# Attention and convolution on one core: GpSimd in program order, the first inner sums of a projection made in the one ahead of it, and parts of k's weights prepared over a longer stretch

## The chip, the cores and the metric

The kernel runs on one core of a Trainium2 chip. The metric is the device time of one execution in microseconds (us), and the median over runs is compared. TensorE (PE in the profile) multiplies, VectorE (DVE), ScalarE (ACT) and GpSimd (POOL) work on elements, and SyncE (SP) and GpSimd issue the transfers between the memory outside the core (DRAM here) and the core's own (SBUF). PSUM holds the sums that TensorE makes.

## The reference

Four images of 1024 channels and 32 x 32 pixels, that is four batches of 1024 tokens, go through an attention layer and then through a convolution block. All is float32.

```python
x = hidden_states.reshape(B, C, N).transpose(0, 2, 1)
qkv = (x @ w_qkv.T + b_qkv).reshape(B, N, 3, nh, hd)
q, k, v = (qkv[:, :, 0], qkv[:, :, 1], qkv[:, :, 2])
q = _rmsnorm(_apply_rope(q, cos, sin).reshape(B, N, inner), q_norm_w).reshape(B, N, nh, hd)
k = _rmsnorm(_apply_rope(k, cos, sin).reshape(B, N, inner), k_norm_w).reshape(B, N, nh, hd)
attn = jax.nn.softmax(jnp.einsum('bqhd,bkhd->bhqk', q, k) * scale, axis=-1)
out = jnp.einsum('bhqk,bkhd->bqhd', attn, v).reshape(B, N, inner) @ w_proj.T
out = _rmsnorm(out, norm_out_w) + x
...
out = relu(_bn(_conv(out1, w1, b1, 1, 0), g1, be1))
out = relu(_bn(_conv(out, w2, b2, 1, 1), g2, be2))
out = relu(out1 + softplus(residual_scale)[0] * _bn(_conv(out, w3, b3, 1, 0), g3, be3))
```

The second part is a 1x1, a 3x3 and a 1x1 convolution with batch norms over all four images. It lies after everything that the change touches.

## The kernel before, in words

**Stages.** For each batch b = 0 to 3 TensorE works through five stages: the projections q, k and v, the attention, and the output projection, which the profile calls y (its sums are p_y). Below, q_1 is the q projection of batch 1, and so on. The convolutions come after y_3.

**Projections.** A 1024 x 1024 x 1024 product is done with seven products of halves in place of eight (Strassen's scheme in Winograd's form). For b = 0 that is one level, `project`: 28 units of 8 matmuls, weights from `operands` (L224), which makes sums of weight blocks on VectorE and stores them in a DRAM tensor wd (L242). For b > 0 each of the seven products is again done with seven, `project2` (L422): 49 products of 8 matmuls. k = 0 to 6 counts the seven outer ones. Their weight parts were prepared once, by `prepare` (L400): it loads four quarters, makes four sums on VectorE (`make`, L407 to L410) and stores them into the DRAM tensor wd2 (L412) through GpSimd's queue. The parts for q, v and y are prepared in the attention of batches 0 and 1; those for k (outer 1 to 6) in y_0, by lines L1015 and L1016, every 4 units, with `make` 3 units after the loads. Their temporaries are `big_temp` tiles, of which there are three; the rotation of q and k (`rope`) and the inverses of the softmax use the same three.

**Inner sums.** Each outer product also needs four sums of the right-hand operand, t1 to t4 (`inner`, L453; VectorE instructions L457 to L461). For k = 0 they stand at the start of the projection, for k + 1 they are made during k. `room` says where they lie, `spare` where partial results of the last two outer products lie. For q and k both are parts of a tile with 16 units (`beside`, L651); it is the tile of y's right-hand sums of the batch before, called `room`, `to` in the profile. `room(k)` there returns almost the same four units for every k. v is a tile of its own, allocated under the same tag "v" in a pool with one buffer (L604), so it takes the memory of `to` once that is released; its inner sums lie in v itself (`in_place`).

**Weights in flight.** Weight parts are loaded by SP into a ring of eight chunks of 256 KB (`wring`), seven per outer product, so a load can be issued when the product seven or eight places before it is through.

**Normalization and residual.** `o_norm` scales y (L818), eight tiles of 128 x 1024 elements for one batch, and stores each into the DRAM tensor x1d through GpSimd's queue (L819). This happens in the stage q of the next batch. The residual, x of that batch, is then added to x1d by transfers that add in DRAM (L976 with `accum_op`, GpSimd's queue, eight of 512 KB). In the program's text these stand at the head of the attention of the next batch, after v.

**What sets the order.** PE's order is that of the program (`manual_schedule`, L91); so is the order of VectorE and ScalarE from L928 on. The order on GpSimd and SP is made by a scheduler with a cost model. `after(n, step)` puts a step n products later in the text, `waiting` holds steps that are let in as VectorE has room, and `product_done` counts.

Of the kernel before, what the change touches and what calls it, by code (L numbers as in the profile page):

```python
# [11 lines left out]
F32 = mybir.dt.float32  # L12
AF = mybir.ActivationFunctionType
ALU = mybir.AluOpType
# [4 lines left out]
P = 128  # L19
B, C, H, W = 4, 1024, 32, 32  # L20
N = H * W
# [64 lines left out]
def program(ctx, tc, x, wblk, w2, w3, vecs, cos, sin, out, bad):  # L86
# [1 line left out]

    nc = tc.nc
    u = "f" if bad is not None else "s"  # L90
    ctx.enter_context(tc.manual_schedule(engines={mybir.EngineType.PE}))  # L91

    const = ctx.enter_context(tc.tile_pool(name=f"const{u}", bufs=1))
    dram = ctx.enter_context(tc.tile_pool(name=f"dram{u}", bufs=1, space=DRAM))
# [58 lines left out]
    with tc.tile_pool(name=f"st{u}", bufs=2) as st, ExitStack() as s:  # L153
# [61 lines left out]
        def flat(t):  # L215
            return t.rearrange("p a b -> p (a b)")
# [34 lines left out]
        def spend(cost):  # L251
            pace["room"] -= cost

        def after(n, step):
            later.append((pace["at"] + n, step))
# [133 lines left out]
        def quarter(t, base, k, oq, iq):  # L389
# [8 lines left out]
            nc.sync.dma_start(t.rearrange("p (g f) -> p g f", g=2), src.rearrange("g p f -> p g f"))  # L398

        def prepare(which, base, k, alloc):  # L400

            a11, a12, a21, a22 = a = alloc(f"pre_{which}_{k}")
            for i, t in enumerate(a):
                quarter(t, base, k, i // 2, i % 2)

            def make():
                nc.vector.tensor_tensor(a22, a21, a22, ALU.add)  # L407
                nc.vector.tensor_tensor(a21, a11, a21, ALU.subtract)
                nc.vector.tensor_tensor(a11, a22, a11, ALU.subtract)
                nc.vector.tensor_tensor(a12, a12, a11, ALU.subtract)  # L410
# [11 lines left out]
        def project2(b, which, base, right, room, spare, dest, tokens, tag, ready):  # L422

# [26 lines left out]
            def b_(k, iq, tq):  # L450
                return right(k, iq, tq)

            def inner(k, part):  # L453
                t1, t2, t3, t4 = t_[k] = room(k)
                spend(2 * TT)
                if part == 0:
                    nc.vector.tensor_tensor(t1, b_(k, 0, 1), b_(k, 0, 0), ALU.subtract)  # L457
                    nc.vector.tensor_tensor(t2, b_(k, 1, 1), t1, ALU.subtract)
                else:
                    nc.vector.tensor_tensor(t3, b_(k, 1, 1), b_(k, 0, 1), ALU.subtract)  # L460
                    nc.vector.tensor_tensor(t4, b_(k, 1, 0), t2, ALU.subtract)  # L461

            def bank2(kind, name):
                return bank(kind, name).rearrange("p (q e) -> p q e", q=2)
# [49 lines left out]
                after(2 * H2, lambda: add_to(k, 0, 0, o))  # L514
                product_done(H2)

            inner(0, 0)
            inner(0, 1)
            start(0)
            second(0)  # L520
            for k in range(len(OUTER)):
                more = k + 1 < len(OUTER)

                pace["hold"] = tokens and not more
                o = banks_[k][0]
                mm(o, w[k][2], t_[k][1], False, False)
                nc.scalar.copy(part(k, 0, 1), o)
                product_done(H2)
                ob = banks_[k][2] = bank2("o2", f"p5_{n}_{k}")
                mm(ob, w[k][3], t_[k][0], True, False)  # L530
                p5 = temp(f"p5_{n}_{k}").rearrange("p (q e) -> p q e", q=2)
                nc.scalar.copy(p5, ob)
                product_done(H2)
                if more:
                    start(k + 1)
                    inner(k + 1, 0)
                mm(o, w[k][4], t_[k][2], False, False)
                nc.scalar.copy(part(k, 1, 1), o)  # L538
                after(2 * H2, lambda k=k, p5=p5: add_to(k, 1, 1, p5))
                product_done(H2)  # L540
                if more:
                    second(k + 1)
                    inner(k + 1, 1)
                mm(ob, w[k][5], b_(k, 1, 1), False, True)
                after(2 * H2, lambda k=k, ob=ob: add_to(k, 0, 1, ob))
                product_done(H2)
                mm(o, w[k][6], t_[k][3], False, True)
                if k > 4:
                    after(2 * H2, lambda k=k, o=o: add(target(k, 1, 0), target(k, 1, 0), o))
# [9 lines left out]
        def qk_proj(b, base, bs, ts, bias, dst, tag, w1=None, two=None, bias_later=False):  # L559
# [36 lines left out]

                    after(0.5 * (i // 2 + 1), done)

            project2(b, two[0], base, two[1], two[2], two[3], dst, False, tag, ready)
            return total  # L600

        def v_proj(b, bs, ts, two=None):

            v = kv.tile([P, N // P, C], F32, tag="v", name=f"v_{b}")  # L604
            if two is not None:
                project2(b, 1, WV, two(v)[0], two(v)[1], two(v)[2], v, True, "v", lambda c: None)
                return v
# [8 lines left out]
            return v  # L616

        def operand(bs, ts):

# [28 lines left out]

            return right, room, spare

        def beside(bs, ts, units):  # L651


            def room(k):
                return units[12], units[13], units[14], units[15 if k % 2 == 0 else 0]

            def spare(k, oq, tq):
                return units[1 + k % 2] if (oq, tq) == (0, 1) else units[3 + oq]

            return operand(bs, ts), room, spare  # L660

# [261 lines left out]
        def v_room(name):  # L923
            return kv.tile([P, N // P, C], F32, tag="v", name=name)

        vector_and_act = {mybir.EngineType.DVE, mybir.EngineType.Activation}
        regions = ExitStack()
        regions.enter_context(tc.manual_schedule(engines=vector_and_act))  # L928
# [10 lines left out]
        queue_sums(ts[0], xs[0])  # L939
        room = v_room("rq_0")  # L940
        for b in range(B):
            units = [flat(room[:, i // 2 : i // 2 + 1, :])[:, half[i % 2]] for i in range(16)]
            units = [t.rearrange("p (q e) -> p q e", q=2) for t in units]
            q_all = kv.tile([P, NT, N], F32, tag="q", name=f"q_{b}")
            two = (0, *beside(xs[b], ts[b], units)) if b > 0 else None
            tq = qk_proj(b, WQ, xs[b], ts[b], "bq", q_all, "q", w1 if b == 0 else None, two, True)
            rope(b, q_all, tq, eps_q, HD / C, None, "q", b == 0)
            k_all = kp.tile([P, NT, N], F32, tag="k", name=f"k_{b}")
            two = (3, *beside(xs[b], ts[b], units)) if b > 0 else None
            tk = qk_proj(b, WK, xs[b], ts[b], "bk", k_all, "k", None, two)  # L950
            rope(b, k_all, tk, eps_rms, 1.0 / C, (wqk_other, wqk), "k")
            v = v_proj(b, xs[b], ts[b], (lambda v, b=b: in_place(xs[b], ts[b], v, True)) if b > 0 else None)

            rest(leave=4 if b > 0 else 0)
            psum_for("att")
# [41 lines left out]
            if b + 1 < B:  # L997
                xs[b + 1] = x_tile(b + 1)
                ts[b + 1] = t_tiles(b + 1)
                rows = (0, 1, 4, 5, 2, 3, 6, 7)  # L1000
                for j in range(NT):

                    def load(b=b, i=rows[j]):
                        for c in range(NCH):
                            load_x(b + 1, c, (i,))

                    after(3 + 1.5 * j, load)
                for i in range(0, NH, 2):
# [368 lines left out]
```

## Time and profile before

| what | value |
|---|---|
| median of 3 runs | 2767.21 us (2765.55 to 2784.42) |
| the profiled execution's own time | 2769.46 us |
| its span | 2767.7 us |
| granted TensorE clock, mean | 0.993 |
| busy: PE, DVE, ACT, POOL | 98%, 76%, 39%, 14% |
| transfers: SP's queue (q1), GpSimd's queue (q0) | 36.2%, 16.3% of 16 engines' span |

The starts of the stages on TensorE, in us from the span's start, are read from the sequence of matmuls in the timeline:

| batch | q | k | v | attention | y |
|---|---|---|---|---|---|
| 0 | 4.91 | 104.11 | 201.01 | 302.66 | 535.99 |
| 1 | 647.38 | 739.76 | 826.57 | 915.37 | 1148.69 |
| 2 | 1233.47 | 1329.24 | 1416.06 | 1504.04 | 1737.37 |
| 3 | 1822.15 | 1919.18 | 2005.99 | 2095.60 | 2329.51 |

The convolutions begin at 2414.22. Names in the profile: p_q, p_k, p_v and p_y are the sums of the projections, pa, pb and pc those of batch 0; sc and cx are the two matmuls of the attention, den the sums of its exponentials on VectorE, ks and qs the rotated halves of k and q, in flight to be added to k and q. "SPq" is the time for which SP is held at an issue of a transfer.

### The profile page before, as it was taken

What the parts mean: (1) busy time and instruction counts of PE and PEld (TensorE: products, weight loads), DVE (VectorE), ACT (ScalarE), POOL (GpSimd) and SP (SyncE); (2) the same over time, 40 slices, a digit from 0 to 9 for tenths busy, and PEclk for the clock granted to TensorE, in tenths of its full rate; (3) what the DMA queues carried; (4) which work ended last, traced back from release to release, by engine and by line L of the source; (5) the groups of instructions that cost most, each with busy time, mean ns of one, the idle gap of its engine ahead of it and who ended that gap; (6) DMA issues with size and microseconds to landing.
All of it is one profiled execution on the core that took longest, in us unless ns stands there. A gap on an engine that the chain in (4) does not pass through costs nothing.

```text
span 2767.7 us, 32938 instructions
## 1 busy us (share of the span) xinstructions
PE 2702.5 (98%) x11746; PEld 1657.4 (60%) x11746; DVE 2095.3 (76%) x2406; ACT 1080.2 (39%) x1494; POOL 383.6 (14%) x447
## 2 busy tenths in 40 slices
PE   9999999989999999999999999999999999999997
PEld 4449533337888433587887333887885335846853
DVE  4355599866688899886788877986888887646987
ACT  1221455413343555432343555232424554212266
POOL 1023023221111122101111110101111111000000
PEclk9999999999999999999999999999999999999999
DMA  5376254586867335359666210668674113672165
GB/s 206 107 186 187 84 168 152 172 307 202 229 189 212 86 111 164 114 169 247 184 187 173 62 24 16 198 193 212 189 218 121 24 24 98 193 261 88 62 215 212
DMA packets 242860, 432.05 MB, mean 156 GB/s; under 512 B 27072, under 2 KB 122608, under 8 KB 242688
## 3 DMA queue, kind: packets, MB, share of 16 engines
q1 hardware_dynamic: 209312, 318.59, 36.2%
q0 software_dynamic: 33376, 111.27, 16.3%
q8 instruction: 96, 1.57, 0.2%
q14 instruction: 76, 0.62, 0.1%
HBM read 295.22 MB, written 96.78 MB: 142 GB/s over the span
## 4 chain that ended last, share of the span: by engine, by line
PE 88%; DMA 5%; DVE 2%; ACT 2%; issue 1%; SPq 0%; POOL 0%; POOLq 0%; DVEq 0%; ACTq 0%
PE sc L758 16%; PE cx L775 16%; PE p_y L448 9%; PE p_v L443 8%; PE p_q L448 8%; PE p_k L448 7%; PE c L847 4%; PE c L1281 4%; PE pa_v L312 2%; PE pa_q L304 2%; DMA w_q<-wdf 2%; PE pa_k L304 2%; PE c2x L1142 2%; PE c2y L1142 2%; PE dn L796 1%
## 5 line engine op out<-in xcount | busy, mean ns | idle before, releaser
L769 DVE TENSOR_TENSOR den<-den,p 128x1024 f32<-128x1024 f32 x384 | 470.5, 1225 | 40.4 <-ACT p L765 0.5
L765 ACT ACTIVATE p<-sc 128x1024 f32<-128x1024 f32 x512 | 476.1, 1045 | 55.7 <-PE sc L758 55.7
L758 PE MATMUL sc<-q,k 64*128 64x512 f32 x2048 | 457.1, 596 | 3.0 <-DVE v L475 2.3
L775 PE MATMUL cx<-p,v 128*64 128x512 f32 x2048 | 453.6, 595 | 0.0
L758 PEld LDWEIGHTS sc<-q,k 64*128 64x128 f32 x2048 | 191.2, 186 | 266.8 <-issue 121.5
L775 PEld LDWEIGHTS cx<-p,v 128*64 128x64 f32 x2048 | 141.4, 137 | 304.3 <-issue 304.3
L739 POOL TENSOR_SCALAR q<-q,vec 128x512 f32<-128x512 f32 x64 | 127.3, 1995 | 537.0 <-DVE q L738 537.0
L780 ACT COPY q<-cx 128x512 f32<-128x512 f32 x64 | 37.5, 586 | 357.3 <-PE cx L775 357.3
L443 PE MATMUL p_v<-w_v,x 128*128 128x256 f32 x696 | 157.5, 379 | 0.2 <-DMA w_v<-wdf 0.2
L448 PE MATMUL p_y<-q,w_y 128*128 128x256 f32 x696 | 157.5, 380 | 0.0
L448 PE MATMUL p_k<-to,w_k 128*128 128x256 f32 x672 | 153.1, 381 | 2.3 <-ACT k L538 1.5
L448 PE MATMUL p_q<-to,w_q 128*128 128x256 f32 x672 | 153.9, 382 | 0.0
L448 PEld LDWEIGHTS p_y<-q,w_y 128*128 128x128 f32 x696 | 131.8, 190 | 20.7 <-issue 2.5
L443 PEld LDWEIGHTS p_v<-w_v,x 128*128 128x128 f32 x696 | 132.1, 190 | 18.8 <-DMA w_v<-wdf 0.9
L448 PEld LDWEIGHTS p_k<-to,w_k 128*128 128x128 f32 x672 | 126.7, 190 | 23.5 <-ACT to L538 2.8
L448 PEld LDWEIGHTS p_q<-to,w_q 128*128 128x128 f32 x672 | 128.8, 192 | 19.4 <-issue 1.6
L767 DVE TENSOR_TENSOR den<-p 128x1024 f32<-128x1024 f32 x64 | 76.5, 1195 | 76.0 <-ACT p L765 76.0
L802 DVE RECIPROCAL rec<-dn 128x512 f32<-128x512 f32 x32 | 107.2, 3349 | 14.4 <-PE dn L796 14.4
L1281 PE MATMUL c<-h,w 128*128 128x512 f32 x256 | 110.3, 592 | 0.9 <-ACT h L1185 0.9
L705 POOL DMA_DIRECT2D q<-qs x64 | 55.7, 1020 | 289.5 <-issue 170.7
L705 POOL DMA_DIRECT2D k<-ks x64 | 55.3, 1002 | 264.4 <-ACT p L765 104.9
L1281 PEld LDWEIGHTS c<-h,w 128*128 128x128 f32 x256 | 48.6, 190 | 62.1 <-issue 54.3
(521 smaller groups left out, 4183.8 us busy)
## 6 DMA issues: line engine op xcount, KB each, us to landing
wd2f<-w_pre POOLq DMA_DIRECT2D x88, 256.0 KB, 2.8
w_q<-wd2f SPq DMA_DIRECT2D x84, 256.0 KB
w_k<-wd2f SPq DMA_DIRECT2D x84, 256.0 KB
w_v<-wd2f SPq DMA_DIRECT2D x84, 256.0 KB
w_y<-wd2f SPq DMA_DIRECT2D x84, 256.0 KB
x<-in_x_dram SPq DMA_DIRECT2D x64, 256.0 KB
q<-qs POOLq DMA_DIRECT2D x64, 256.0 KB, 5.4
k<-ks POOLq DMA_DIRECT2D x64, 256.0 KB, 4.2
```

The lines of the kernel that those rows point to most:

```text
L304: nc.tensor.matmul(o, w[:, i, :], r(i), start=first and i == 0, stop=last and i == NH - 1, skip_group_check=True,)
L443: nc.tensor.matmul(o[:, q].rearrange("p (g f) -> p g f", g=2), r[:, i, q * P : (q + 1) * P], wt[:, :, i, :], skip_group_check=True, **at,)
L448: nc.tensor.matmul(o[:, q], wt[:, q, i, :], r[:, i, :], skip_group_check=True, **at)
L705: nc.gpsimd.dma_start(dst[i::2, f, :], other[1 - i :: 2, :], accum_op=ALU.add)
L739: nc.gpsimd.tensor_scalar(cx, cx, col("bv", hp), None, ALU.add)
L758: nc.tensor.matmul(sc[:, j], k_all[d, hp, t * P : (t + 1) * P], q_all[d, hp, at], start=True, stop=bad is not None,)
L765: nc.scalar.activation(p, sc, AF.Exp)
L769: nc.vector.tensor_tensor(d_, d_, p, ALU.add)
L775: nc.tensor.matmul(o[j * HD : (j + 1) * HD, :], v[:, t, h0 : h0 + HD], probs[t][:, j], start=(t == 0), stop=(t == N // P - 1),)
L847: nc.tensor.matmul(o, w[f][ih][:, ii, :], ys[:, i, half[c]], start=(i == 0), stop=(i == NT - 1))
L1142: nc.tensor.matmul(o[:, r * TR * TC : (r + 1) * TR * TC], uw[2 * h + r, j][:, i * PL + f * P : i * PL + (f + 1) * P], vt[b, i][:, 2 * h + ...
L1281: nc.tensor.matmul(os[i], w3t[k][f // NH][:, f % NH, :], h2[b, k][:, half[c]], start=(k == 0), stop=(k == NPT - 1),)
```

## The change

- GpSimd too is held to the program's order (the first hunk).
- Inner sums: `inner_sums` is taken out of `project2`. The sums for k = 0 of a projection are made in the last outer product of the projection ahead, through the list `ahead`: those of q in y of the batch before, those of k in q, those of v in k. A projection makes them itself only where `first` is true: q_1 and the three y.
- `beside` alternates between units 8 to 11 and 12 to 15 for the sums, and the spare parts lie in units 0, 2, 4 and 6.
- v is no tile of its own: it is written into `room`.
- The preparation of k's parts in y_0 is spread: a part every 5 units in place of every 4, `make` 4 units after the loads in place of 3, and the loads are issued on GpSimd's queue in place of SP's.

```diff
-    ctx.enter_context(tc.manual_schedule(engines={mybir.EngineType.PE}))
+    ctx.enter_context(tc.manual_schedule(engines={mybir.EngineType.PE, mybir.EngineType.Pool}))
...
-        def prepare(which, base, k, alloc):
+        def prepare(which, base, k, alloc, queue=nc.sync):
...
-                quarter(t, base, k, i // 2, i % 2)
+                quarter(t, base, k, i // 2, i % 2, queue)
...
+        def inner_sums(right, room, k, part):
+            t1, t2, t3, t4 = room(k)
+            spend(2 * TT)
+            if part == 0:
+                nc.vector.tensor_tensor(t1, right(k, 0, 1), right(k, 0, 0), ALU.subtract)
+                nc.vector.tensor_tensor(t2, right(k, 1, 1), t1, ALU.subtract)
+            else:
+                nc.vector.tensor_tensor(t3, right(k, 1, 1), right(k, 0, 1), ALU.subtract)
+                nc.vector.tensor_tensor(t4, right(k, 1, 0), t2, ALU.subtract)
+        ahead = []
...
-            inner(0, 0)
-            inner(0, 1)
+            t_[0] = room(0)
+            if first:
+                inner(0, 0)
+                inner(0, 1)
...
                 if more:
                     start(k + 1)
                     inner(k + 1, 0)
+                elif ahead:
+                    inner_sums(*ahead[0], 0, 0)
...
                 if more:
                     second(k + 1)
                     inner(k + 1, 1)
+                elif ahead:
+                    inner_sums(*ahead.pop(), 0, 1)
...
-        def v_proj(b, bs, ts, two=None):
+        def v_proj(b, bs, ts, v, two=None):
-            v = kv.tile([P, N // P, C], F32, tag="v", name=f"v_{b}")
...
-        def beside(bs, ts, units):
+        def beside(bs, ts, units, odd):
             def room(k):
-                return units[12], units[13], units[14], units[15 if k % 2 == 0 else 0]
+                at = 8 + 4 * ((k + odd) % 2)
+                return units[at : at + 4]
             def spare(k, oq, tq):
-                return units[1 + k % 2] if (oq, tq) == (0, 1) else units[3 + oq]
+                return units[2 * (k % 2)] if (oq, tq) == (0, 1) else units[4 + 2 * oq]
...
-            two = (0, *beside(xs[b], ts[b], units)) if b > 0 else None
+            two2 = None
+            if b > 0:
+                two2 = [beside(xs[b], ts[b], units, odd) for odd in (1, 0)]
+                two2.append(in_place(xs[b], ts[b], room, True))
+                ahead.append(two2[1][:2])
+            two = (0, *two2[0], b == 1) if b > 0 else None
...
+            if b > 0:
+                ahead.append(two2[2][:2])
...
-            v = v_proj(b, xs[b], ts[b], (lambda v, b=b: in_place(xs[b], ts[b], v, True)) if b > 0 else None)
+            v = room
+            v_proj(b, xs[b], ts[b], v, (*two2[2], False) if b > 0 else None)
...
-                        after(4 * k - 3.5, lambda k=k: after(3, prepare(3, WK, k, big_pieces)))
+                        after(5 * k - 4.5, lambda k=k: after(4, prepare(3, WK, k, big_pieces, nc.gpsimd)))
...
-            two = (2, *in_place(q_all, tc_, yt[b], False)) if b > 0 else None
+            two = None
+            if b > 0:
+                two = (2, *in_place(q_all, tc_, yt[b], False), True)
+                if b + 1 < B:
+                    ahead.append(beside(xs[b + 1], ts[b + 1], units_of(room), 1)[:2])
```

More of the change, by code (lines that the diff above doesn't have):

```diff
@@ L387, in quarters, with quarter @@
             return of[:, 4 * ob + 2 * oq : 4 * ob + 2 * oq + 2, tb * CH + tq * QT : tb * CH + (tq + 1) * QT]
-        def quarter(t, base, k, oq, iq):
+        def quarter(t, base, k, oq, iq, queue=nc.sync):
             ob, ih = {"A11": (0, 0), "A12": (0, 1), "A22": (1, 1)}.get(OUTER[k], (None, None))
@@ L397, in quarter @@
                 src = wblk[at : at + 2][:, :, ih * CH + iq * QT : ih * CH + (iq + 1) * QT]
-            nc.sync.dma_start(t.rearrange("p (g f) -> p g f", g=2), src.rearrange("g p f -> p g f"))
-        def prepare(which, base, k, alloc):
+            queue.dma_start(t.rearrange("p (g f) -> p g f", g=2), src.rearrange("g p f -> p g f"))
+        def prepare(which, base, k, alloc, queue=nc.sync):
             a11, a12, a21, a22 = a = alloc(f"pre_{which}_{k}")
             for i, t in enumerate(a):
-                quarter(t, base, k, i // 2, i % 2)
+                quarter(t, base, k, i // 2, i % 2, queue)
             def make():
@@ L420, in big_pieces, with project2 @@
             return [t[:, h] for t in (big_temp(f"{name}_{i}") for i in range(2)) for h in half]
-        def project2(b, which, base, right, room, spare, dest, tokens, tag, ready):
+        def inner_sums(right, room, k, part):
[8 more added lines that the diff above has]
+        ahead = []
+        def project2(b, which, base, right, room, spare, first, dest, tokens, tag, ready):
             n, H2 = f"{tag}_{b}", 0.5
@@ L453, in inner @@
             def inner(k, part):
[L454 to L461, printed above, removed]
+                t_[k] = room(k)
+                inner_sums(right, room, k, part)
             def bank2(kind, name):
@@ L597, in ready @@
                     after(0.5 * (i // 2 + 1), done)
-            project2(b, two[0], base, two[1], two[2], two[3], dst, False, tag, ready)
+            project2(b, two[0], base, *two[1:], dst, False, tag, ready)
             return total
-        def v_proj(b, bs, ts, two=None):
-            v = kv.tile([P, N // P, C], F32, tag="v", name=f"v_{b}")
+        def v_proj(b, bs, ts, v, two=None):
             if two is not None:
-                project2(b, 1, WV, two(v)[0], two(v)[1], two(v)[2], v, True, "v", lambda c: None)
-                return v
+                project2(b, 1, WV, *two, v, True, "v", lambda c: None)
+                return
             def outs(g):
@@ L615, in v_proj @@
             project(b, WV, bs, ts, outs, None, lambda *a, **k: None, True, "v")
-            return v
         def operand(bs, ts):
@@ L924, in v_room, with units_of @@
             return kv.tile([P, N // P, C], F32, tag="v", name=name)
+        def units_of(room):
+            units = [flat(room[:, i // 2 : i // 2 + 1, :])[:, half[i % 2]] for i in range(16)]
+            return [t.rearrange("p (q e) -> p q e", q=2) for t in units]
         vector_and_act = {mybir.EngineType.DVE, mybir.EngineType.Activation}
@@ L941, in program @@
         for b in range(B):
-            units = [flat(room[:, i // 2 : i // 2 + 1, :])[:, half[i % 2]] for i in range(16)]
-            units = [t.rearrange("p (q e) -> p q e", q=2) for t in units]
+            units = units_of(room)
             q_all = kv.tile([P, NT, N], F32, tag="q", name=f"q_{b}")
-            two = (0, *beside(xs[b], ts[b], units)) if b > 0 else None
+            two2 = None
[4 more added lines that the diff above has]
+            two = (0, *two2[0], b == 1) if b > 0 else None
             tq = qk_proj(b, WQ, xs[b], ts[b], "bq", q_all, "q", w1 if b == 0 else None, two, True)
@@ L948, in program @@
             k_all = kp.tile([P, NT, N], F32, tag="k", name=f"k_{b}")
-            two = (3, *beside(xs[b], ts[b], units)) if b > 0 else None
+            if b > 0:
+                ahead.append(two2[2][:2])
+            two = (3, *two2[1], False) if b > 0 else None
             tk = qk_proj(b, WK, xs[b], ts[b], "bk", k_all, "k", None, two)
             rope(b, k_all, tk, eps_rms, 1.0 / C, (wqk_other, wqk), "k")
-            v = v_proj(b, xs[b], ts[b], (lambda v, b=b: in_place(xs[b], ts[b], v, True)) if b > 0 else None)
+            v = room
+            v_proj(b, xs[b], ts[b], v, (*two2[2], False) if b > 0 else None)
             rest(leave=4 if b > 0 else 0)
```

## Prediction

> **What bounds the kernel now.** The page first: PE is busy for 2702.5 of 2767.7 us (98%) and the chain that ended last is 88% PE. A change can win only where PE stands still, or where it runs slowly because it stood still. So the second view is PE's waits, for the whole span; of its 15 rows these are the ones that the change can reach:
>
> ```profile
> PE p_q L448 <- DMA w_q<-wdf: 18.4, 5, 5.0
> PE pa_y L304 <- DVE w_y_0b L238: 4.7, 1, 4.7
> PE pa_y L304 <- ACT y L323: 3.4, 1, 3.4
> PE p_v L443 <- ACT k L594: 2.2, 3, 0.7
> PE p_q L448 <- DMA w_q<-in_wblk_dram: 2.1, 2, 1.1
> PE pa_y L304 <- DVE w_y_1b L238: 1.1, 1, 1.1
> PE pa_y L304 <- DVE w_y_2b L238: 1.0, 1, 1.0
> ```
>
> The columns are us in total, times, longest. Weights that arrive late in q (20.5 us, q_1 to q_3) lead, then y_0 with 10.2 us, then the start of v (2.2 us). Third, PE in order of time at the largest wait of q_2:
>
> ```profile
> 1272.23 5.34 PE L448 MATMUL p_q<-to,w_q 128*128 128x256 f32 x24
> 1282.53 3.78 PE L448 MATMUL p_q<-t,w_q 128*128 128x256 f32 x8 [4.96 <-DMA w_q<-wdf]
> 1286.11 2.26 PE L448 MATMUL p_q<-to,w_q 128*128 128x256 f32 x8
> ```
>
> Eight matmuls are 1.73 us apart elsewhere; after the wait they take 3.58 and 2.09. A wait of 5 us costs over 7. Fourth, POOL's queue at the same place:
>
> ```profile
> 1263.92 0.91 POOL L976 DMA_DIRECT2D x1df<-in_x_dram  x1 [1.08 <-DMA x1df<-y]
> 1267.15 1.81 POOL L976 DMA_DIRECT2D x1df<-in_x_dram  x2 [2.31 <-DMA x1df<-y]
> 1268.69 0.84 POOL L819 DMA_DIRECT2D x1df<-y  x1
> 1282.23 0.83 POOL L976 DMA_DIRECT2D x1df<-in_x_dram  x1 [12.70 <-DMA x1df<-y]
> ```
>
> The scheduler has drawn the adding transfers of the residual (L976) from the attention up into q, between the stores of y. PE's wait ends at 1282.5, when the store behind three of them has landed. Last, busy times by stage: q_2, k_2, the attention of batch 1, y_0.
>
> ```profile
> core 0: us, PE busy (x) PEld busy (x) DVE busy (x) ACT busy (x) POOL busy (x), PEclk, DMA share, GB/s
> 1233.50:1329.20 95.70, 88.16 (x401) 75.81 (x400) 68.31 (x91) 30.06 (x51) 12.27 (x18) 0.96 0.84 229
> 1329.20:1416.10 86.90, 86.15 (x402) 74.28 (x402) 70.48 (x92) 36.05 (x61) 8.07 (x10) 1.00 0.66 180
> 915.40:1148.70 233.30, 233.30 (x1089) 84.49 (x1089) 205.93 (x175) 128.91 (x145) 51.15 (x53) 1.00 0.36 99
> 536.00:647.40 111.40, 101.17 (x229) 43.83 (x226) 66.64 (x85) 18.63 (x32) 29.96 (x48) 0.95 0.78 267
> ```
>
> q and k have the same matmuls; with a DMA share of 0.66 k never waits for weights, q with 0.84 does. The attention has no idle PE and an idle DMA.
>
> **What the Trainium skill says.** "DMA: Bandwidth & Descriptors", section "Issuing engines are not separate DMA queues": transfers issued by SP and GpSimd run on the same 16 engines and interleave. The trace agrees: from 1237 to 1327 q0 takes 44.6% and q1 40.9% of them. So k's loads moved to POOL still load the same engines; only what they hold up on SP goes. "PSUM — Partial Sum Buffer", section "Engine vs sequencer instructions": GpSimd's queue is a strict FIFO; the 12.70 us above, with stores of y behind it, agree. "TensorE: Matmul & The Clock Gate", section "What's actually happening": the clock halves after an idle window of about 3.4 us; here it was 0.50 from 1280 to 1285.
>
> **The change part by part.** The order of instructions of the two builds says what moves: PE and ACT keep theirs exactly; DVE's differs in y_0 and by the inner sums; on POOL all eight L976 of a batch now stand behind ks_3, at the head of the attention, and the eight stores of y in front.
>
> *Residual out of q (gain 29).* Without waits q is 49 products of 1.727 us plus 0.57 for the sum of squares: 85.2. The stages take 92.4, 95.8 and 97.0 (starts of the matmuls), 29.6 over in sum. Does enough traffic leave? q0 works 0.446 of 90 us = 40 us here. The broadcast of y's sum is 2.5 (estimate: q0 in k is 13.7 us, less 11.2 for as many bytes of rotated halves as the 32 us from 918 to 950 show). Stores: in y_0 q0 moves 10.49 MB in 0.348 x 80 us, so 4.2 MB of y are about 11 us. The eight adding transfers are left with about 26 us, 3.2 each (my estimate; the trace never shows them alone; at least 1.25 for 0.5 MB at the highest rate that the DMA view shows, 419 GB/s from 560 to 640, at most 5, as three and a store took 17 us). Then q's share becomes about (40 - 26 + 37)/85 = 0.6, below k's 0.66. Bounds: 0, if y's stores alone delay the weights, and 29.6. I take 29.
>
> *Residual into the attention (cost 0).* It costs 26 us of DMA, from about 923 in batch 1, where the share is near 0 until 945. POOL issues eight at 0.83. Behind them stand k<-ks of the rows 4 to 7, issued at 932 to 976 as VectorE makes them. Row 4 would now land near 953 in place of 936. TensorE wants it at the fifth head pair, 915.4 + 4 x 14.6 = 974. VectorE wants its temporary (one of three) back for ks_6 at 957.0: 4 us left, and VectorE idles 2.17 us at 961.8. So cover is about 6 us a batch. Without it each us is paid three times. Low end -3 (late by a little), taken 0.
>
> *v into the room of the sums, inner sums ahead (gain 2).* Before, VectorE begins v's first sum only at 829.39, and PE, which needs the second at 830.81, starts at 830.91: 0.72, 0.73, 0.73. Now they are made in k. The wait is put down to ACT L594, but DVE's order shows the sum. Four sums (2.7 us) of q, k and v move, none is added: DVE is busy 70 of 87 us there, and PE at the starts of q and k waits for nothing. Bounds 0 and 2.2, plus up to 2 if the alternating units also end the waits of k (L538, 2.3 in sum).
>
> *y_0 (gain 6).* 28 units of 3.433 us are 96.1; the stage takes 111.4, so 15.3 are lost: 4.7 and 2.6 of slow matmuls, 1.1, 1.1, 3.4 and 1.5 slow, crumbs. First wait: VectorE makes w_y_0b at 566.17 after 1.51 of waiting for its load, issued by SP at 557.5 behind k's loads. These leave SP: about 1.5 less; the rest comes from the late inverses and stays. Second and third: w_y_1b and w_y_2b's last loads stand on SP behind k's loads, which wait there for temporaries (582.2, 598.3 to 601.2); gone, 2.2. Fourth: `make` of part 4 (2.7 us) stood ahead of the sum that ScalarE waits for; now behind: 2.7 and the 1.5. Sum 7.9. Against it: POOL, now in order, holds the stores of w_y behind loads that wait for a temporary. Each issue is 0.5 to 1 us, 24 more; w_y's next load needs the store, but the sum needs the chunk only after the fourth product (13.7 us later). I take 6; bounds -8 (every group late by 2) and 11.
>
> Sum: 29 + 0 + 2 + 6 = 37. The profiled execution's own time is 2769.5 (span 2767.7 and 1.8 around it), so 2732.5; it lies 2.3 over the median of the runs, so 2730.
>
> **The rivals.**
> *A, partly:* stores of y still delay weights, or y_0 wins nothing. For it: at 1260 to 1265, with three stores in flight, the share is 0.97 already. Against: no wait falls there, and later stores come 3 to 12 us apart. Half of q gone and v: 14.5 + 2, so 2750.
> *B, no effect:* the weights are late because of the ring of eight chunks, not traffic. Against: k has the same ring and no wait. Gain of 2 and 3: 2762.
> *C, slower:* VectorE stalls at ks_6 in the attention since row 4 is stuck behind the adding transfers. For it: VectorE is busy 206 of 233 us and PE has no slack. It decides when the eight take more than 26 + 6 us: each us beyond costs 3. It eats all 37 at 12 us beyond (5.5 each, above my bound of 5), and gives 2790 at 20 beyond.
>
> **How the numbers follow.** Forecast 0.70 (2720 to 2741), A 0.20 (2741 to 2757), B 0.05, C 0.05. The range 2720 to 2757 leaves out B, C and the ends. 1% is 27.7 us, about what a measurement of this kernel can tell from no change: under 2739.5 is nearly all of the forecast, 0.67. A, B and the forecast's tail are within 1%: 0.28. C: 0.05.
>
> **What would show it.** Right: no L976 in q; q_1 to q_3 each 85 to 86.5 us, with a DMA share of 0.6; L976 in a row at the start of the attention, its share there near 1 for 25 us, PE still without a wait; p_v's wait for L594 gone; y_0 near 105 us. Wrong: w_q<-wdf still among PE's waits (A, B); DVE waiting for k<-ks in the attention for over 5 us (C); POOL waiting for its own stores in y_0 while VectorE waits for w_y.

## The result, and the profile after

The changed kernel takes 2732.06 us (median of six runs, 2728.4 to 2734.88) against 2768.77 for the kernel before (six runs, 2765.23 to 2784.42). The ratio is 0.9859, with a 95% interval of 0.9834 to 0.9883. The forecast was 2730. The profiled execution has a span of 2733.0 us and, at 2734.88 in all, is the longest of its six.

Lines move in the changed kernel: L443 is L456 now, L448 is L461, L705 is L717, L819 is L831 and L976 is L1000. The stages, as differences of their starts on TensorE in the profiled executions, in us:

| stage | before | after | gain | forecast |
|---|---|---|---|---|
| q_1, q_2, q_3 | 92.4, 95.8, 97.0 | 85.6, 85.7, 85.7 | 28.2 | 29 |
| v_1, v_2, v_3 | 88.8, 88.0, 89.6 | 88.2, 89.3, 88.9 | 0.0 | 2 |
| attention, all four | 233.3, 233.3, 233.3, 233.9 | the same | 0.0 | 0 |
| y_0 | 111.4 | 103.8 | 7.6 | 6 |
| y_1, y_2 | 84.8, 84.8 | 85.0, 85.6 | -1.0 | none |
| start of the convolutions | 2414.2 | 2379.2 | 35.0 | 37 |

TensorE's waits over the whole span, in the changed kernel (us in total, times, longest):

```profile
PE p_v L456 <- DMA w_v<-wdf: 6.0, 6, 1.8
...
PE pa_y L304 <- issue: 3.8, 1, 3.8
...
PE p_y L461 <- DMA w_y<-wdf: 0.6, 1, 0.6
PE pa_y L304 <- DVE w_y_1b L238: 0.3, 1, 0.3
```

The rows of p_q, 20.5 us before, are gone. So is p_v's wait for ScalarE's L594 (2.2), but p_v's wait for weights has grown from 3.4 to 6.0. In y_0 one wait of 3.8 and one of 0.3 are left of four. Busy times of q_2, k_2, the attention of batch 1 and y_0, with the same columns as before:

```profile
1218.40:1304.10 85.70, 85.65 (x402) 74.48 (x401) 68.09 (x91) 30.09 (x51) 5.43 (x10) 1.00 0.65 206
1304.10:1390.90 86.80, 86.04 (x401) 74.30 (x400) 70.29 (x92) 36.14 (x61) 8.09 (x10) 1.00 0.66 181
900.10:1133.40 233.30, 233.30 (x1089) 84.49 (x1089) 205.41 (x175) 128.92 (x145) 58.74 (x61) 1.00 0.45 117
535.70:639.45 103.75, 99.64 (x228) 43.48 (x225) 63.67 (x81) 18.73 (x32) 43.46 (x66) 0.97 0.78 263
```

q_2's share of the DMA engines fell from 0.84 to 0.65, and the attention's rose from 0.36 to 0.45, with TensorE busy in all of it as before. GpSimd's queue at the head of that attention shows what moved:

```profile
906.65 7.43 POOL L1000 DMA_DIRECT2D x1df<-in_x_dram  x8
917.22 0.85 POOL L717 DMA_DIRECT2D k<-ks  x1 [3.13 <-DVE k L711]
918.93 0.84 POOL L717 DMA_DIRECT2D k<-ks  x1 [0.86 <-DMA x1df<-in_x_dram]
```

The eight adding transfers are issued in a row, and the halves of row 4 of k come behind them. In slices of 5 us the share (the last column but one) then stays above 1 until 936 (it is the sum of the packets' times, and these can overlap):

```profile
931.00:936.00 5.00, 5.00 (x26) 2.11 (x22) 4.79 (x4) 5.00 (x7) 0.26 (x1) 1.00 1.06 206
936.00:941.00 5.00, 5.00 (x24) 1.64 (x24) 4.58 (x5) 1.85 (x3) 0.00 (x0) 1.00 0.56 138
941.00:946.00 5.00, 5.00 (x25) 1.85 (x23) 3.26 (x3) 2.10 (x3) 1.17 (x2) 1.00 0.00 0
```

VectorE takes row 4's temporary for ks_6 at 941.70 and has not waited for it. Row 4's second half had landed at 936.48, the last of row 5 at 939.52, so the move was free with about 5 us to spare.

### The profile page after: what moved, and what is told of

Its sections match the earlier page's. It is cut to its first block, busy times and chain, and to the rows that moved or that the text cites. A ratio compares the mean times of both kernels' runs of the same rounds, so it can differ in the third digit from the quotient of the medians.

```text
span 2733.0 us, 32908 instructions
## 1 busy us (share of the span) xinstructions
PE 2692.9 (99%) x11746; PEld 1652.8 (60%) x11746; DVE 2091.9 (77%) x2406; ACT 1081.1 (40%) x1494; POOL 403.3 (15%) x471
## 3 DMA queue, kind: packets, MB, share of 16 engines
q0 software_dynamic: 35296, 117.56, 16.7%
## 4 chain that ended last, share of the span: by engine, by line
PE 92%; DMA 3%; DVE 2%; ACT 2%; issue 0%; SPq 0%; POOL 0%; ACTq 0%; POOLq 0%; DVEq 0%
PE sc L770 17%; PE cx L787 16%; PE p_q L461 9%; PE p_y L461 9%; PE p_v L456 8%; PE p_k L461 7%; PE c L859 4%; PE c L1309 4%; PE pa_q L304 2%; PE pa_v L312 2%; PE pa_k L304 2%; PE c2x L1170 2%; PE c2y L1170 2%; DMA w_v<-wdf 2%; PE pa_y L304 2%; PE dn L808 1%
## 5 line engine op out<-in xcount | busy, mean ns | idle before, releaser
L787 PE MATMUL cx<-p,to 128*64 128x512 f32 x1536 | 340.2, 595 | 0.0
L787 PEld LDWEIGHTS cx<-p,to 128*64 128x64 f32 x1536 | 106.0, 137 | 228.3 <-issue 228.3
L456 PE MATMUL p_v<-w_v,x 128*128 128x256 f32 x696 | 157.9, 379 | 1.9 <-DMA w_v<-wdf 1.9
L461 PE MATMUL p_y<-q,w_y 128*128 128x256 f32 x696 | 157.5, 380 | 0.0
L461 PE MATMUL p_k<-to,w_k 128*128 128x256 f32 x672 | 153.1, 381 | 2.3 <-ACT k L549 1.5
L461 PE MATMUL p_q<-to,w_q 128*128 128x256 f32 x672 | 152.5, 380 | 0.1
L456 PEld LDWEIGHTS p_v<-w_v,x 128*128 128x128 f32 x696 | 132.0, 190 | 21.0 <-DMA w_v<-wdf 3.1
L461 PEld LDWEIGHTS p_y<-q,w_y 128*128 128x128 f32 x696 | 131.8, 190 | 20.7 <-issue 2.5
L461 PEld LDWEIGHTS p_k<-to,w_k 128*128 128x128 f32 x672 | 126.7, 190 | 23.5 <-ACT to L549 2.8
L461 PEld LDWEIGHTS p_q<-to,w_q 128*128 128x128 f32 x672 | 127.2, 190 | 19.5 <-issue 1.6
L787 PE MATMUL cx<-p,rq 128*64 128x512 f32 x512 | 113.4, 595 | 0.0
L717 POOL DMA_DIRECT2D q<-qs x64 | 55.6, 1020 | 289.6 <-issue 190.8
L717 POOL DMA_DIRECT2D k<-ks x64 | 55.2, 997 | 242.1 <-ACT p L777 91.1
```

The source lines that it names most:

```text
L456: nc.tensor.matmul(o[:, q].rearrange("p (g f) -> p g f", g=2), r[:, i, q * P : (q + 1) * P], wt[:, :, i, :], skip_group_check=True, **at,)
L461: nc.tensor.matmul(o[:, q], wt[:, q, i, :], r[:, i, :], skip_group_check=True, **at)
L717: nc.gpsimd.dma_start(dst[i::2, f, :], other[1 - i :: 2, :], accum_op=ALU.add)
L787: nc.tensor.matmul(o[j * HD : (j + 1) * HD, :], v[:, t, h0 : h0 + HD], probs[t][:, j], start=(t == 0), stop=(t == N // P - 1),)
```

## The experiments

All are timed in the same way as the changed kernel, each against runs of the kernel before on the same chip. Stages are read from one profiled execution of each.

### GpSimd's order alone, and everything but that order

The kernel before with the first hunk alone:

```diff
-    ctx.enter_context(tc.manual_schedule(engines={mybir.EngineType.PE}))
+    ctx.enter_context(tc.manual_schedule(engines={mybir.EngineType.PE, mybir.EngineType.Pool}))
```

> The kernel before with only the first hunk: GpSimd in program order. Theory (the residual's order makes the gain of q): the eight adding transfers leave q, so q_1, q_2 and q_3 take 85.6 us each as in the changed kernel (28.2 less than before in sum); y_0 and v stay as before (111.4 and 88.0 to 89.6). Time about 2739. Rival (the parts of k's weights or the inner sums relieve q): q keeps most of its 92 to 97 us, time above 2755.

Measured: 2738.75, ratio 0.9877 (0.9860 to 0.9893). q_1 to q_3 take 85.6, 85.4 and 85.4; v keeps its wait for L594 and sums to 267.1; y_0 takes 108.8. One line of the change makes q's whole gain, and by it the convolutions start 30.5 us earlier, of the 35.0 of the whole change.

The changed kernel with the same line taken back:

> The changed kernel without its first hunk: GpSimd's order by the scheduler. The adding transfers stand between the stores of y in q again. Theory: q_1 to q_3 take 92 to 97 us as before, and y_0 keeps its 103.8 us, since its gain is from the way k's parts are spread: time about 2760. Rival (y_0's gain needs GpSimd's program order): y_0 at 108 or more, time 2765 or more.

Measured: 2764.94, ratio 0.9969 (0.9953 to 0.9984). q takes 93.1, 96.7 and 97.9, with 21.2 us of waits for w_q, and y_0 104.1. The time is 5 us above the 2760 expected: q is slower here than in the kernel before (287.7 for 285.2 in sum), and the kernel before is itself at 2771.39 in the runs that this one is compared with. Both parts of the theory hold: q's gain needs the order, y_0's gain does not.

### The inner sums and v's room alone

The kernel before with the inner sums made ahead, `beside` and v in `room`; GpSimd's order and k's parts as before.

> The kernel before with only the inner sums made ahead and v in the room; GpSimd's order by the scheduler, k's parts as before. Theory (v is held by its transfers, so that the wait freed at its start comes back as waits for w_v): the wait of 0.7 us at p_v's start is gone in each batch, w_v waits grow from 3.4 to about 6 in sum, and the three stages v stay at 266.4 in sum, plus or minus 1. q stays at 92 to 97. Time 2767, plus or minus 2. Rival (the growth of the w_v waits comes from GpSimd's order or k's parts): v's three stages sum to 264 and the time is 2765.

Measured: 2776.24, ratio 1.0018 (1.0010 to 1.0026), so a little slower than the kernel before (2771.39 here), which neither side expected. v's three stages sum to 264.6 in place of 266.4, with 4.1 us of waits for w_v: just outside the theory's range, and nearer to the rival's 264. What was lost lies in q_1 (100.5 for 92.4; a second weight wait of 3.16 us and slow matmuls behind it) and y_0 (113.1 for 111.4). Why the inner sums lengthen these under the scheduler's order was not followed up.

v needs more than one profile. Eleven of the kernels here make the inner sums ahead and keep v's other work (all but the kernel before, the one with GpSimd's order alone and the one without the second tables): v sums to 262.8 to 266.4 in them, 264.9 in the mean. The two without it have 266.4 and 267.1. The gain is 1.9 in the mean (against a mean of only two), and 0.0 in the changed kernel's own profile is one end of the scatter.

### k's parts loaded by SyncE again

```diff
-    after(5 * k - 4.5, lambda k=k: after(4, prepare(3, WK, k, big_pieces, nc.gpsimd)))
+    after(5 * k - 4.5, lambda k=k: after(4, prepare(3, WK, k, big_pieces)))
```

> The changed kernel with one edit: the loads of k's parts on SyncE's queue again, still a part every 5 units. Theory of the prediction: taking them off SyncE was worth 1.5 and 2.2 us, so y_0 takes 107.5 in place of 103.8 and the time is 2736. Rival: the spread alone makes the gain, y_0 within 0.7 us of 103.8 and the time 2732.

Measured: 2730.36, ratio 0.9839 (0.9823 to 0.9856); y_0 takes 103.6. In sum it makes no difference which queue loads the parts. Spreading them (5 units in place of 4, the sums 4 units after the loads in place of 3) is what took away the second to fourth waits of y_0: the run without GpSimd's order has none of them and 104.1, and it differs from the run with the inner sums alone, with all of them and 113.1, in k's parts only.

For the first wait the queue does make a difference, in two ways that cancel. The sums of w_y_0b on VectorE, with k's loads on SyncE and then, in the changed kernel, on GpSimd:

```profile
565.67 0.69 DVE L236 TENSOR_TENSOR w_y_0b_s<-w_y_0b,w_y_0b 128x512 f32<-128x512 f32 x1 [2.11 <-DMA w_y_0b<-in_wblk_dram]
564.95 0.68 DVE L236 TENSOR_TENSOR w_y_0b_s<-w_y_0b,w_y_0b 128x512 f32<-128x512 f32 x1
```

On GpSimd's queue the wait for w_y_0b's load is gone. But the first part's loads go out there at 540.05, 4.4 us after the start of y_0, and land from 546 to 551, while SyncE moves the inverses of the softmax. VectorE's last product with an inverse then starts 18.4 to 19.3 us after the start of y_0 (the changed kernel and the six variants below that keep these loads as they are), and 16.7 to 17.0 us after it in the two kernels with the loads on SyncE, where these stand behind the inverses.

### The residual in other places

First in q again, but in program order, each adding transfer behind its own store (the loop at the head of the attention, not shown, is taken out):

```diff
                 nc.gpsimd.dma_start(x1d[f, :, b * N : (b + 1) * N], y)
+                nc.gpsimd.dma_start(x1d[f, :, b * N : (b + 1) * N], x[b, f * P : (f + 1) * P, :], accum_op=ALU.add)
```

> The changed kernel, GpSimd in program order, but with each adding transfer of the residual written directly behind the store of y that it adds to, in stage q. Theory (it is the residual's transfers in q that delay the weights, whoever orders them): p_q waits for w_q again, q_1 to q_3 take 92 to 97 us each, time about 2760. Rival (other moves in GpSimd's program order make the gain of q): q stays at 86 to 87, time 2732.

Measured: 2787.11, ratio 1.0053 (1.0033 to 1.0073), slower than the kernel before; yet q takes 85.7 three times and has no wait for weights. The loss is in k, at 105.4, 107.1 and 106.3:

```profile
PE p_k L461 <- ACT k L515: 50.7, 3, 17.4
```

Each adding transfer waits at the head of GpSimd's queue for its store, with the next store behind it. The last store of y_1 goes out at 1334.5, in k_2. k has the memory of y (both are tiles of tag "k"), so ScalarE cannot write k before 1342.06. That is a new wait, and it says nothing for either theory; that q has none, with a DMA share of 0.88, 0.81 and 0.82 in q_1 to q_3 (0.92 to 0.94 from the first store on), speaks against the first, although in q_2 only five of the eight adding transfers still fall into q.

Second in k, spread, one every 7 us (again with the loop taken out):

```diff
+                    after(4 + 2 * f, add_x)
```

> The changed kernel with the residual's eight adding transfers in stage k, one every two units (7 us), in place of the head of the attention. They bring about 22 us of transfers (4.2 of the 6.0 MB that GpSimd's queue moves in 34 us there), so k's share rises from 0.66 to about 0.92. Theory (what decides is the share of the stage, not the stage): k, now 86.8 us, gets waits for w_k of 4 us or more in each batch and takes 91 to 95, time 2745 to 2760. Rival (only a burst together with the stores of y delays weights): k stays under 88, time 2732 to 2736.

Measured: 2766.53, ratio 0.9984 (0.9976 to 0.9992). k takes 100.6, 98.7 and 98.9, with 27.7 us of waits for w_k in all. So another stage suffers in the same way, and more than expected, but at a share of only 0.77. In the trace the adding transfers come out in groups with the rotated halves of q, which add as well: two and two, four in flight.

These two together break the theory that the share of a stage decides. The queues' packets show more. Here are the two queues (packets, MB, share of 16 engines; q0 is GpSimd's, q1 is SyncE's with the weights) in the 12 us from 1266 to 1278, first in the kernel before, ahead of q_2's wait of 4.96 us:

```profile
q0 software_dynamic: 497, 1.82, 80.4%
q1 hardware_dynamic: 526, 0.88, 22.7%
```

then in the kernel with a store and its adding transfer in turn:

```profile
q1 hardware_dynamic: 1501, 1.93, 47.4%
q0 software_dynamic: 294, 1.07, 46.3%
```

When several of GpSimd's transfers are in flight the queues have about as many packets each (497 to 526), as if they took turns. The Trainium skill has such turns: by "DMA: Bandwidth & Descriptors", section "Queues, rings and completion order", each DMA engine goes round the queues that have work "at *packet* granularity". Its packets are larger, typically 9 to 17 descriptors; those that this trace counts are single pieces of at most 4 KB, and it is in these that the counts are about even. GpSimd's hold 3.7 KB in the mean (1.82 MB by 497) and the weights' 1.7 KB, and in time it is 80 to 23. Seven chunks of 256 KB are 1.83 MB for one outer product of 12.1 us. The weights got 0.88 MB in 12 us; with two transfers in flight they got 1.93.

### The same bytes, in a burst and paced

Four of the eight adding transfers in q, the other four at the head of the attention. Once the four are issued in a row behind four stores, once each behind its own store (the index ranges are shortened to `...`):

```diff
+                for g in range(4) if f == 3 else ():
+                    nc.gpsimd.dma_start(x1d[g, ...], x[b, ...], accum_op=ALU.add)
```

```diff
+                if f < 4:
+                    nc.gpsimd.dma_start(x1d[f, ...], x[b, ...], accum_op=ALU.add)
```

> The changed kernel with half of the residual in stage q: four stores of y, then the four adding transfers to them one behind the other, then the other four stores; the other four adding transfers stay at the head of the attention. The last run but one of this kind (a store and its adding transfer in turn, eight of them) left q without a wait at shares of 0.9 to 0.97, so the share of a stage does not decide. New theory (transfers of GpSimd's queue that are in flight together starve the weights, a few at a time do not): p_q waits 3 us or more for w_q in each batch, q_1 to q_3 take 89 to 96 us, time about 2750. Rival (12 transfers of 16 in q are few enough, however they are grouped): q at 86, time 2732.

> The same four adding transfers in stage q, so the same bytes, but each directly behind its own store, so that it waits for that store and one store and one adding transfer are in flight. Theory (in flight together): p_q has no wait for w_q, q_1 to q_3 at 85.7, time 2730 to 2736. Rival (bytes decide): q as long as in the run with the four in a row.

Measured: in a row 2755.6, ratio 0.9943 (0.9922 to 0.9964), with q at 93.6, 93.4 and 93.3; paced 2734.77, ratio 0.9863 (0.9836 to 0.9890), with q at 85.6, 93.1 and 85.7. The bytes are the same. q_2 in a row:

```profile
1224.60:1318.00 93.40, 88.76 (x402) 76.41 (x401) 68.16 (x91) 30.17 (x51) 8.94 (x14) 0.96 0.72 211
```

and q_1, q_2 and q_3 paced:

```profile
639.70:725.20 85.50, 85.50 (x401) 74.39 (x400) 68.92 (x92) 30.10 (x51) 13.32 (x21) 1.00 0.89 261
1218.90:1311.90 93.00, 88.84 (x401) 76.20 (x400) 68.35 (x91) 30.27 (x51) 8.95 (x14) 0.96 0.75 212
1806.80:1892.50 85.70, 85.66 (x402) 74.48 (x401) 68.09 (x91) 30.06 (x51) 8.99 (x14) 1.00 0.80 231
```

So the same bytes cost 8 us in a burst, and a stage at 0.89 loses nothing where one at 0.72 loses 8 us. In the burst, from 1264 to 1276, the weights got 0.48 MB in 12 us:

```profile
q0 software_dynamic: 536, 1.95, 89.1%
q1 hardware_dynamic: 485, 0.48, 15.2%
```

The theory had no wait for any of the three stages, so q_2 of the paced kernel is a miss. It is a burst too. GpSimd was held up by the fourth adding transfer, and the last four stores went out in a row behind it, at 1279.97. From 1280 to 1290 the two queues read:

```profile
q0 software_dynamic: 500, 1.85, 78.8%
q1 hardware_dynamic: 631, 0.66, 19.1%
```

and the wait of 3.84 us ends at 1291.78. So four stores in a row beside one adding transfer can delay weights too. They lie near the limit: in q_1 and q_3 four stores go out in a row as well, and there is no wait (in q_1 the weights got 0.88 MB in the 10 us behind 703.5, here 0.66). In q_2 TensorE had waited 0.28 us for weights at 1279.08, just before the burst, so the lead of the ring was used up when it began; in q_1 and q_3 it had not waited. The number in flight is thus not enough to tell whether a wait comes. The profiled execution of the paced kernel, at 2741.63, is the longest of its four, and two of the others, at 2732, leave little room for such a wait.

### The residual twice

```diff
-                for f in range(NT):
+                for f in [f for f in range(NT) for _ in range(2)]:
```

> The changed kernel with every adding transfer issued twice at the head of the attention, so that x is added twice. It tests the cover of the attention. Transfers of 45 us stand ahead of the rotated halves of k's rows 4 to 7. By the prediction the cover ends at 32 us: VectorE waits at ks_6 for its temporary about 13 us a batch, TensorE follows, and the time is 2732 + 3 x 13 = 2771. Rival (the cover is larger, as VectorE has not waited there at all with the eight): attention stays at 233.3, time 2732 to 2736.

Measured: 2883.45, ratio 1.0399 (1.0375 to 1.0423). The attention of batches 1 to 3 takes 284.6, 284.3 and 286.0. For batch 1, VectorE's wait and then TensorE's:

```profile
DVE ks L711 <- DMA k<-ks: 52.8, 1, 52.8
```

```profile
PE dn L808 <- DVE den L781: 47.9, 1, 47.9
```

The place and the price are those of rival C: VectorE stops at ks_6, and 52.8 us there make the stage 51.3 longer. The amount expected, 13, was far too small. The second transfer to a row has to wait for the first, so GpSimd's queue was held for 78 us (906.0 to 984.2) and not for the transfers' own time. With at most two in flight, from 955 to 985, 3.15 MB, six of them, take 0.638 of 30 us: 3.2 us each, 51 for all sixteen.

### Where y_0's first wait comes from

In the kernel with k's parts on SyncE, the sums of the first part 6 units after its loads:

```diff
+    after(5 * k - 4.5, lambda k=k: after(4 if k > 1 else 6, prepare(3, WK, k, big_pieces)))
```

> The kernel of the run with k's parts on SyncE's queue, with one edit: the sums of the first part are made 6 units after its loads in place of 4, so that they stand behind the sums of w_y_0b on VectorE. Theory (the first wait of y_0, 4 us and 2.8 of slow matmuls, comes from these 2.8 us of sums ahead): the wait falls to 1.3 or less, y_0 takes 98 to 100 in place of 103.6, time 2726. Rival (the later parts, whose temporaries come free later, are held up and hold w_y_1b or w_y_2b): y_0 at 103 or more.

Measured: 2738.71, ratio 0.9882 (0.9862 to 0.9902); y_0 takes 109.7. The first wait falls from 4.1 to 2.6, not to 1.3, since VectorE now waits 3.1 us for w_y_0b's own load, and one of 5.6 for w_y_1b appears: the rival. The first part now holds its temporaries too long for the second: VectorE waits 8.67 us for the second's loads until 580.4, and the sums of w_y_1b stand behind it, at 588.45. So all parts were moved by the same amount:

```diff
-    after(5 * k - 4.5, lambda k=k: after(4, prepare(3, WK, k, big_pieces, nc.gpsimd)))
+    after(5 * k - 2.5, lambda k=k: after(4, prepare(3, WK, k, big_pieces, nc.gpsimd)))
```

> The changed kernel with one number changed: each part of k's weights starts 2 units later (5k - 2.5 in place of 5k - 4.5), all by the same amount, so that the sums of every part stand behind those of w_y_0b, w_y_1b, ... on VectorE and no temporary is held longer. Theory (the first wait of y_0 comes from the 2.8 us of the first part's sums ahead of w_y_0b): this wait falls from 3.8 to about 1, the slow matmuls behind it go, y_0 takes 98 to 100 in place of 103.8, time about 2727. Rival (the wait comes from the late inverses and loads alone): y_0 stays within 1 us of 103.8. That the last part falls into q_1 should cost nothing.

Measured: 2726.20 (2725.35 to 2727.15), ratio 0.9836 (0.9814 to 0.9858); y_0 takes 97.2, close to its 96.1 without any wait. The first product with w_y_0b in the changed kernel, and in this one:

```profile
567.19 6.54 PE L304 MATMUL pa_y<-to,w_y_0b 128*128 128x512 f32 x8 [3.78 <-issue]
```

```profile
563.76 3.60 PE L304 MATMUL pa_y<-to,w_y_0b 128*128 128x512 f32 x8
```

The wait is gone, and so are the 2.9 us by which the eight matmuls were slower after it. But the edit moved two things. The sums of w_y_0b start 24.6 us after the start of y_0, for 29.3 in the changed kernel: 2.8 of these 4.7 us are the first part's sums, which now stand behind, and 1.9 are the inverses, which come at 16.7 us again: the first part's loads go out at 556.07, behind them. By the sums alone about 1 us of the wait would have stayed (an estimate: 3.8 less 2.8), as the theory had it. This is the fastest version that computes the whole reference: its runs all lie below those of the changed kernel, though the two were not timed together.

### v without the second load of the tables

The kernel leaves out a load that the result needs, to see what it costs.

> The changed kernel without the reload of the tables of cosines and sines between the rotation of q and that of k for batches 1 to 3 (left out: k is rotated with tables that still carry q's norm). It takes 1 MB, or three transfers on SyncE's queue among the weights, out of stage v. Theory (v's second wait for w_v, 0.7 to 1.8 us, is from these transfers beside the rotated halves): that wait is gone, the first one of 0.6 to 0.7, ahead of the tables, stays; v's three stages sum to 262 in place of 266.4, time about 2728. Rival (the ring or the rotated halves alone): both waits stay, v at 265 to 267.

Measured: 2727.50, ratio 0.9839 (0.9812 to 0.9865). v takes 87.0, 87.1 and 87.5, 261.6 in sum. The first wait for w_v stays (0.47, 0.47 and 0.93), and the second, 0.69, 1.84 and 1.50 in the changed kernel, is gone from all three: the theory. Of the 6.0 us of waits for w_v 1.9 are left. How much of v's time these tables take is less sure: the kernel with k's parts two units later, which does load them, has 262.8 in its one profile, only 1.2 more.

## Why the prediction was right, and where its reasons were wrong

**Residual out of q: 29 forecast, 28.2 measured, and the gain needs GpSimd's order alone (first experiment). The reason given was wrong in one point.** The step compared shares: "with a DMA share of 0.66 k never waits for weights, q with 0.84 does", and asked "Does enough traffic leave?" The runs with four adding transfers show that the share does not decide: no wait at 0.89, 4.6 us of waiting at 0.72. What fits the runs is that the weights starve when several of GpSimd's transfers are in flight together, while the ring of eight chunks has a lead of at most 13.8 us (eight products of 1.727). It is not a full account: four stores in a row delayed q_2 of the paced kernel and not its q_1 and q_3, and the number in flight was not varied apart from what GpSimd's queue moves in some 10 us. The forecast came out right because moving the residual removes the groups as well as the bytes; as far as it rests on the share, that is luck. By its own argument the run with the residual in q in turn would have had weight waits, and it has none.

The transfers' price, 3.2 us each by estimate, was somewhat too high for where they went. GpSimd's queue in the attention of batch 1, before and after:

```profile
q0 software_dynamic: 3200, 10.49, 16.4%
q0 software_dynamic: 4352, 14.68, 26.0%
```

That is 9.6% of 233.3 us for 4.2 MB, 22 us for eight or 2.8 each, and in the row they land 2.5 us apart (916.17, 918.65, 921.14 and so on to 931.09). 3.2 is what they take with two in flight (the residual twice).

**Residual into the attention: 0 forecast, 0 measured.** VectorE has no wait for k<-ks there. The cover was put at about 6 us, 4 of it until the temporary is needed. The trace shows 5.2: row 4 has landed at 936.48, the need is at 941.70. Rival C's chain is real, as the run with the residual twice shows, and its price of one us for one us in each batch holds (52.8 and 51.3).

**v and the inner sums: 2 forecast, 0.0 in the profile, 1.9 in the mean of eleven.** The wait that was to go is gone; later weight waits take between nothing and all of it. The step did not ask what is late next in v. It is the weights, in part behind the tables.

**y_0: 6 forecast, 7.6 measured, with wrong terms.** The 2.2 of the second and third wait were put down to SyncE's queue; with the loads back on SyncE these waits are still gone, so they are an effect of the spread. "These leave SP: about 1.5 less" is right for the wait that it names: VectorE no longer waits for w_y_0b's load. But the step left out that on GpSimd's queue these loads go out earlier, beside the inverses, which come 1.9 us later than with the loads on SyncE; the first wait fell by 0.9 only (4.7 to 3.8). And "the rest comes from the late inverses and stays" fell with the last y_0 run: with 2.8 us of sums behind w_y_0b, and the loads out of the inverses' way, all but 0.4 went. VectorE's order was in the trace of the kernel before as well (the sums of the first part from 560.59 on, those of w_y_0b behind them at 566.17; in the changed kernel from 560.97 on and at 564.95). The loss feared from GpSimd, which now holds stores of w_y behind loads, did not appear: y_0 is 103.8 with the loads on GpSimd's queue and 103.6 without them. So the forecast of 6 came near by other terms than its own, which is partly luck.

**What the sum left out:** y_1 and y_2 lose 1.0 together, 0.6 of it waits for w_y. In the sum the misses offset each other in part: 2 less in v, 1.0 less in y_1 and y_2, 0.8 less in q, 1.6 more in y_0. The signs: L976 is out of q, each q is within 85 to 86.5, p_v's wait for L594 is gone, y_0 is near 105. The shares of q_1 to q_3, 0.72, 0.65 and 0.66, are above the 0.6 forecast, and the stretch at a share near 1 in the attention lasts some 30 us, not 25, since the rotated halves of k run in it too.

## What to carry to other kernels

An engine whose order a scheduler makes can draw transfers far ahead of where the program has them, into a stage that needs the bandwidth; look at where they run, not at where they are written. For weights streamed with a short lead, look at the transfers of other queues that are in flight together, and not only at the stage's mean DMA share: the same bytes one by one were free in two stages of three here, and in a burst cost 8 us in all three. And a step that is prepared ahead, its loads too, should stand behind the instruction that the critical engine waits for; two units made 6.6 us here. When transfers move to another queue, ask when they will now start, and beside what.

## What the runs showed of the hardware

With several of GpSimd's transfers in flight, its queue and that of the weights had about as many packets each (497 to 526, 536 to 485; with stores in the burst 500 to 631), so the one whose packets take longer got the time: in the burst 0.32 us for 3.6 KB against 0.06 us for 1.0 KB made 89% against 15%. Size is not all of it: the adding packets took longer than plain ones. In y_0 of the kernel before (560 to 640), where GpSimd's queue adds nothing, 3200 packets of 3.3 KB took 34.8% of 16 engines, 0.14 us each; in the run with the residual twice (955 to 985) 866 of 3.6 KB took 63.8%, 0.35 us each. The plain ones come from SBUF and the adding ones from DRAM; what of the difference is the adding is not shown. Larger packets for the weights may even this out; that was not tried.

An adding transfer of 512 KB from DRAM into DRAM took 3.2 us of all engines with two in flight (164 GB/s), and in a row of eight they landed 2.5 us apart (210 GB/s). Slices of 2 us in y_0 of the kernel before reach 419.
